# A graph-attention layer on one NeuronCore: the clearing of the accumulators, the depth of the statistics, one comparison's operand and the last batches' chunk size are changed

## The chip, the core and the metric

The kernel runs on one core of one Trainium2 chip. The metric is the device time of one execution in microseconds (us). Engines are named as in the profile: PE (TensorE, with PEld for its weight loads), DVE (VectorE), ACT (ScalarE), POOL (GpSimd) and SP (SyncE, which here only issues DMAs).

## The reference, cut to what matters

There are 12500 nodes with 128 features, and 412500 edges, sorted by target node, with 64 features each. Four heads of 32 columns attend over the edges that enter a node.

```python
h = relu(layernorm(x))                                   # per node
hw = (h @ W_node.T).reshape(n, 4, 32)
e = (edge_attr_64 @ W_edge.T).reshape(edges, 4, 32)
att = sum(concat([hw[src], hw[dst], e]) * a)             # per edge and head
att = where(att > 0, att, 0.2 * att)
m = maximum(segment_max(att, dst), 0)
ex = exp(att - m[dst])
denom = segment_sum(ex, dst) + (edges - deg) * exp(-m)
out = x + segment_sum(ex / denom[dst] * hw[src], dst)
```

## The kernel before, in words

**Node table.** The first stage normalizes the nodes and multiplies them with one prepared matrix (`wall`), and writes 98 blocks of 128 rows to `table` in HBM. A row has 144 numbers: per head 32 projected columns, two ones and the source's share of the attention, and behind them the target's shares. Blocks come in groups (3, 6, then mostly 9 blocks: one load of `xg`, one write of the table) and in units of three blocks. The order on every engine is written out by hand (`tc.manual_schedule()`): loop step `k` issues the product of unit `k` (`project`, `keep_rows`), the normalizing and the transposes of unit `k+2` (`normalize`, `turn`, `keep_turned`) and the statistics of unit `k+ahead` (`measure`). When a group's last unit is measured, the next steps take its square root on ACT (`root`, L282) and its reciprocal and shift on DVE (`deviate`, L287 and L289). Step `k == 4` issues the loads of `load_extents` (L215), and four later steps the POOL subtraction `find_rise` (L225). Ahead of the loop, the first `ahead - 2` units are measured.

**Extents.** After the table, `extent` and about 25 short DVE instructions (L230 to L444) work out where every chunk of edges begins and ends among the nodes. One result is `nid`, the node number that a partition stands for in each group of four chunks.

**Edges.** Edges come in chunks of 896 (7 tiles of 128), eight chunks to a batch, 58 batches; the last has five chunks and 31 tiles. `gather` issues one indirect DMA on POOL for each tile (L497), which fetches 128 rows of the table: 3223 in all. `hs` has two buffers. In the iteration of batch `b` the gathers of batch `b+1` are issued, then `weigh(b)` (attention, running maxima, exponentials), `scatter(b)` (rows times weights on DVE, L575; a product with the one-hot `hot` on PE, L583; `collect` copies the sums out on ACT, L606), `begin(b+1)` (edge scores of the next batch on PE), and after every second batch `merge` (into the accumulators `acc`, L653). Of the last two batches each has a merge of its own. `finish` divides, adds `x`, and writes groups of nodes that are complete.

`scatter` takes chunks in steps of `G` = 3: three chunks' rows are multiplied, then one set of matmuls has 96 columns of `hot` as weights and 420 columns to stream; in the last batch the step is 1 (32 columns as weights, 140 to stream).

`begin` starts with two DVE comparisons of 128x896 each (L510): which edges of a chunk go to which node, as ones and zeros in `mem`. The matmuls L518 then add the targets' shares. Four short instructions on DVE follow (L521 to L527), and the one-hot comparisons (L530).

One PSUM bank, named `exr`, holds small operands: the exponentials (`ex_ps`), a row of numbers (`rows_ps`) and a scratch piece for `finish` (`em_ps`).

`acc` (128x13720 numbers) is cleared by one ACT copy. It is the first statement of the edge stage (L745), but on ACT, where nothing holds it back, it stands first of all computing instructions.

Of the kernel before, what the change touches and what calls it, by code (L numbers as in the profile page):

```python
# [9 lines left out]
F32 = mybir.dt.float32  # L10
BF16 = mybir.dt.bfloat16
I32 = mybir.dt.int32
AF = mybir.ActivationFunctionType
OP = mybir.AluOpType
# [3 lines left out]
P = 128  # L18
N = 12500
D = 128  # L20
# [4 lines left out]
T = 7  # L25
CE = T * P
# [73 lines left out]
def kernel(  # L100
# [77 lines left out]
    with (  # L178
# [62 lines left out]
        def load_rows(b0, n):  # L241

            full = min(n, (N - b0 * P) // P)
            s = Rows()
            s.b0, s.n = b0, n
            s.x = p2.tile([P, XB, D], F32, name="xg", bufs=4)
            nc.sync.dma_start(s.x[:, :full, :],
                              x[b0 * P:(b0 + full) * P, :].rearrange("(b p) d -> p b d", p=P))
            if full < n:
                nc.gpsimd.memset(s.x[:, full, :], 0.0)  # L250
                rest = N - (b0 + full) * P
                nc.sync.dma_start(s.x[:rest, full, :], x[(b0 + full) * P:N, :])
            s.stats = p2.tile([P, XB, 2, 3], F32, name="stats", bufs=4)
            s.units = []
            for i0 in range(0, n, XS):
                u = Rows()
                u.s, u.i0, u.m = s, i0, min(XS, n - i0)
                s.units.append(u)
            return s


        def measure(u):
            s = u.s
            for i in range(u.i0, u.i0 + u.m):
                nc.vector.bn_stats(s.stats[:, i, :, :].rearrange("p a b -> p (a b)"), s.x[:, i, :])  # L265
            if u is not s.units[-1]:
                return

            n = s.n
            tot = p2.tile([P, XB, 2], F32, name="tot", bufs=4)  # L270
            nc.vector.tensor_tensor(tot[:, :n, :], s.stats[:, :n, 0, 1:], s.stats[:, :n, 1, 1:], op=OP.add)  # L271
            dif = p2.tile([P, XB], F32, name="dif", bufs=4)
            nc.vector.tensor_tensor(dif[:, :n], s.stats[:, :n, 0, 1], s.stats[:, :n, 1, 1], op=OP.subtract)
            nc.vector.scalar_tensor_tensor(dif[:, :n], dif[:, :n], D / 4.0, dif[:, :n], op0=OP.mult, op1=OP.mult)
            nc.vector.tensor_tensor(dif[:, :n], dif[:, :n], tot[:, :n, 1], op=OP.add)
            s.mean2, s.var = tot[:, :n, 0], dif[:, :n]
            measured.append(s)

        def root(s):
            n = s.n  # L280
            s.rstd = p2.tile([P, XB], F32, name="rstd", bufs=4)
            nc.scalar.activation(s.rstd[:, :n], s.var, AF.Sqrt, bias=eps, scale=1.0 / D)  # L282
            rooted.append(s)

        def deviate(s):
            n = s.n
            nc.vector.reciprocal(s.rstd[:, :n], s.rstd[:, :n])  # L287
            s.shift = p2.tile([P, XB], F32, name="shift", bufs=4)
            nc.vector.scalar_tensor_tensor(s.shift[:, :n], s.mean2, -0.5, s.rstd[:, :n], op0=OP.mult, op1=OP.mult)  # L289

        def normalize(u):
# [45 lines left out]
                groups.append(s)  # L337
                units.extend(s.units)

        for _ in range(4):  # L340
            load_next()
        ahead = 6
        for u in units[:ahead - 2]:
            for s in rooted:
                deviate(s)
# [18 lines left out]
        while k < len(units):  # L364
# [26 lines left out]
                find_rise(k // 4 - 4)  # L391
            k += 1
        write(full)
        pe = pps.tile([P, H], F32, name="pw", bufs=1)
        nc.tensor.matmul(pe, we.rearrange("p s k -> p (s k)"), a_diag[:, 2, :], start=True, stop=True)
        for s in range(2):
# [54 lines left out]
    ps = stack.enter_context(tc.tile_pool(name="ps", bufs=1, space=bass.MemoryType.PSUM))  # L451


    bank = ps.tile([P, T * R + W + GB * 4], F32, name="exr")
    ex_ps = bank[:, :T * R].rearrange("p (t r) -> p t r", t=T)
    rows_ps = bank[:, T * R:T * R + W]
    em_ps = bank[:, T * R + W:]
    nc.scalar.copy(rows_ps, riota)

    hot = work.tile([P, T, CB, W], F32, name="hot")  # L460

# [44 lines left out]
    def begin(s):  # L506

        for k in range(2):
            pair = 2 * s.b + k
            nc.vector.tensor_scalar(s.mem[:, k, :], s.mem[:, k, :].bitcast(I32), nid[:, pair:pair + 1], None,  # L510
                                    op0=OP.is_equal)
        s.z = ps.tile([R, CE], F32, name="z")
        for part in (slice(0, HALF), slice(HALF, CE)):
            for j in range(SB):
                nc.tensor.matmul(s.z[:, part], wa3[:, j, :], s.eft[:, j, part], start=(j == 0), stop=False)  # L515
        for part in (slice(0, HALF), slice(HALF, CE)):
            for k in range(2):
                nc.tensor.matmul(s.z[:, part], twb[:, s.b % 2, k, :], s.mem[:, k, part], start=False,  # L518
                                 stop=(k == 1))
        dk = work.tile([P, SB * CT], I32, name="dk")  # L520
        nc.vector.tensor_scalar(dk, s.dst, W - 1, None, op0=OP.bitwise_and)  # L521

        key = work.tile([P, SB * CT], F32, name="key")
        nc.vector.tensor_tensor(key.rearrange("p (c t) -> p c t", t=T), s.dst.rearrange("p (c t) -> p c t", t=T),
                                floor[:, s.b * CB:(s.b + 1) * CB, None].to_broadcast([P, CB, T]), op=OP.subtract)
        nc.vector.tensor_scalar(key, key, float(W), float(W), op0=OP.is_ge, op1=OP.mult)
        nc.vector.tensor_tensor(key, key, dk, op=OP.add)  # L527
        for q0 in range(0, s.chunks, 2):
            k = key[:, q0 * T:q0 * T + CT].rearrange("p (q t) -> p q t", t=T)
            nc.vector.tensor_tensor(hot[:, :, q0:q0 + 2, :].rearrange("p t q r -> p q t r"),  # L530
                                    rows_ps[:, None, None, :].to_broadcast([P, 2, T, W]),
                                    k[:, :, :, None].to_broadcast([P, 2, T, W]), op=OP.is_equal)
# [31 lines left out]
    def scatter(s):  # L564


        by_chunk = s.hs[:, :, :EROW].rearrange("p (q t) k -> p q t k", t=T)
        held = [n for j in range(SB) for n in tiles_of(s.b * SB + j)]
        step = G if s.b + 1 < NBT else 1
        for q0 in range(0, s.chunks, step):  # L570
            w = min(step, s.chunks - q0)
            for q in range(q0, q0 + w):
                n = held[q]
                rows = by_chunk[:, q, :n, :].rearrange("p t (h k) -> p t h k", h=H)[:, :, :, :HB]
                nc.vector.tensor_tensor(  # L575
                    rows, rows, ex_ps[:, :n, q * H:(q + 1) * H, None].to_broadcast([P, n, H, HB]), op=OP.mult)
            pa = ps.tile([P, G * H * AW], F32, name="pa", bufs=2)

            n = held[q0 + w - 1]
            order = [0, *range(n, T if w > 1 else n), *range(1, n)]  # L580
            for i in order:
                v = w if i < n else w - 1
                nc.tensor.matmul(pa[:v * W, :v * H * AW], hot[:, i, q0:q0 + v, :].rearrange("p q r -> p (q r)"), by_chunk[:, q0:q0 + v, i, :],  # L583
                                 start=(i == order[0]), stop=(i == order[-1]))
            collect(s, q0, w, pa)
# [156 lines left out]
    with tc.manual_schedule():  # L742
        for b in range(-1, NBT):
            if b == -1:
                nc.scalar.copy(acc.rearrange("p q d -> p (q d)"), carry_m.to_broadcast([P, NQ * AW]))  # L745
                for k in range(2):
                    batch(k).src, batch(k).dst = early[k]
                load_pen(batch(0))
            elif b + 2 < NBT:
                batch(b + 2).src, batch(b + 2).dst = index(b + 2)  # L750
            if b + 1 < NBT:
                load(batch(b + 1))
                gather(batch(b + 1), sums if b >= 1 else None)
            if b >= 0:
                s = batch(b)
                weigh(s)
                if b + 1 < NBT:
                    load_pen(batch(b + 1))
                for store in stores:
                    store()  # L760
                stores.clear()
                scatter(s)
            if b + 1 < NBT:
                begin(batch(b + 1))
            if b >= 0:
                first, last = merge_of(b)
                if b == last:
                    merge(first * CB, chunks_of(first, last))
                del batches[b]
            if b == 3:  # L770
                count_windows()
            for b0, n, behind in parts():
                if behind == b:
                    stores.append(finish(work, ps, "up", em_ps, b0, n))
        for store in stores:
            store()
# [251 lines left out]
```

## Time and profile before

| | |
|---|---|
| median of 3 runs | 4203.52 us (4203.04 to 4205.55) |
| profiled execution | 4203.49 us, its span 4201.7 us |
| first gather starts | 95.19 us after the span's start |
| last gather starts, ends | 4152.28, 4153.23 us |
| L497, gathers on POOL | 3223, mean 954 ns busy |
| L510, comparisons on DVE | 116, mean 672 ns |
| L745, clearing on ACT | 1, 11.62 us |
| busy shares | POOL 74%, DVE 42%, PE 37%, ACT 15% |

A row of the groups reads: line, engine, operation, output<-inputs, shapes, count, then busy time and the mean of one in ns, then the engine's idle time just before them and who ended it. A row of the timeline reads: start, duration (of all that are merged into the row), engine, line, operation, and in brackets the idle time before it and who ended that.

### The profile page before, as it was taken

The numbers are of one execution on the slowest core, as the hardware profiler recorded it, in microseconds if no ns is written. First come the engines' busy times: TensorE is split into PE (matmuls) and PEld (weight loads), VectorE is DVE, ScalarE is ACT, GpSimd is POOL, SyncE is SP. The second block draws the span as 40 slices with busy tenths as digits, with TensorE's granted clock in tenths as the row PEclk, the third lists the DMA queues.
The fourth block names the chain that finished last, engine by engine and source line by source line (L and its number), as shares of the span: only waits on it lengthen the run. The fifth ranks groups of instructions, "written<-read, shape, count | busy, mean of one in ns | idle before, by whom it ended". The sixth has DMA issues, their size and how long they took to land.

```text
span 4201.7 us, 23990 instructions
## 1 busy us (share of the span) xinstructions
PE 1537.7 (37%) x4651; PEld 630.5 (15%) x4651; DVE 1767.9 (42%) x3336; ACT 648.3 (15%) x2553; POOL 3099.8 (74%) x3337
## 2 busy tenths in 40 slices
PE   5324242424342423333333333343334242424243
PEld 4101110111111111111111111111111111111111
DVE  7334353435342534353435343534353434333445
ACT  5111111101110111111111111111111111111111
POOL 2777777777777777777777777777777777777774
PEclk9667676666666766666666667676767676767676
DMA  5333433343333333334333334333333333333331
GB/s 169 114 113 88 130 97 113 93 118 88 118 93 113 97 113 93 118 88 118 93 113 98 113 93 118 88 117 93 113 97 113 93 116 90 115 95 110 100 108 48
DMA packets 243628, 440.90 MB, mean 105 GB/s; under 512 B 93946, under 2 KB 144118, under 8 KB 243478
## 3 DMA queue, kind: packets, MB, share of 16 engines
q0 software_dynamic: 103136, 237.83, 21.6%
q1 hardware_dynamic: 127030, 194.11, 13.8%
q10 hardware_dynamic: 13312, 7.36, 0.6%
q8 instruction: 45, 0.74, 0.1%
q14 instruction: 105, 0.86, 0.1%
HBM read 423.75 MB, written 15.29 MB: 104 GB/s over the span
## 4 chain that ended last, share of the span: by engine, by line
POOL 71%; issue 24%; DVE 2%; DMA 1%; PE 1%; ACT 1%; SPq 0%; POOLq 0%; ACTq 0%; DVEq 0%
POOL hs L497 71%; DMA hs<-table,src 1%; PE pa L583 1%; DVE hT L311 0%; ACT acc L745 0%; DVE stats L265 0%; POOL gate L495 0%; DVE hn L297 0%; PE pt L306 0%; ACT hn L300 0%; PE ph L316 0%; DMA twb<-table 0%; DVE acc L653 0%; DVE tot L271 0%; ACT r L606 0%
## 5 line engine op out<-in xcount | busy, mean ns | idle before, releaser
L497 POOL DMA_INDIRECT hs<-table,src x3223 | 3073.3, 954 | 978.2 <-issue 968.1
L583 PE MATMUL pa<-hs,hot 128*96 128x420 f32 (+2 forms) x2456 | 902.1, 531 | 2465.3 <-issue 2421.5
L583 PEld LDWEIGHTS pa<-hs,hot 128*96 128x96 f32 (+2 forms) x2456 | 413.7, 173 | 2965.6 <-issue 2829.1
L538 DVE STREAM_TRANSPOSE zst<-hs 128x224 f32<-128x224 f32 x58 | 33.6, 579 | 1681.2 <-DMA hs<-table,src 1681.2
L606 ACT COPY r<-pa 32x35 f32<-32x35 f32 x1842 | 385.3, 209 | 819.0 <-PE pa L583 799.1
L575 DVE TENSOR_TENSOR hs<-hs,exr 128x924 f32<-128x924 f32 x461 | 476.8, 1102 | 0.0
L547 ACT ACTIVATE a<-z 32x224 f32<-32x224 f32 x232 | 80.5, 347 | 2087.8 <-DVE z L546 2087.8
L515 PE MATMUL z<-eft,wa 128*32 128x384 f32 (+1 forms) x928 | 361.5, 543 | 21.2 <-DMA twb<-table 21.2
L530 DVE TENSOR_TENSOR hot<-exr,key 128x448 f32<-128x448 f32 x231 | 138.7, 622 | 396.4 <-PE pa L583 394.5
L518 PE MATMUL z<-mem,twb 128*32 128x512 f32 x464 | 185.6, 543 | 5.9 <-DVE mem L510 5.9
L556 ACT ACTIVATE both<-a 32x224 f32<-32x224 f32 x232 | 89.9, 388 | 370.1 <-DVE a L553 365.8
L515 PEld LDWEIGHTS z<-eft,wa 128*32 128x32 f32 x928 | 97.6, 110 | 269.2 <-issue 269.2
L546 DVE TENSOR_TENSOR z<-z,zst 32x224 f32<-32x224 f32 x232 | 89.7, 387 | 81.6 <-ACT a L547 76.2
L653 DVE TENSOR_TENSOR acc<-acc,a 128x70 f32 x461 | 108.3, 235 | 32.9 <-DVE acc L653 18.0
L550 DVE TENSOR_TENSOR_SCAN up<-pen,z 32x896 f32<-32x896 f32 x58 | 117.0, 2016 | 2.0
L552 DVE TENSOR_TENSOR_SCAN m<-pen,up 32x896 f32<-32x896 f32 x58 | 116.4, 2007 | 2.0
L558 DVE SCALAR_TENSOR_TENSOR both<-pen,m 32x224 f32<-32x224 f32 x232 | 88.1, 380 | 2.4
L510 DVE TENSOR_SCALAR mem<-mem,nid 128x896 f32<-128x896 int32 x116 | 73.3, 672 | 21.5 <-DMA mem<-in_dstc 21.5
L718 PE MATMUL up<-a,ident 128*32 128x224 f32 (+2 forms) x480 | 44.0, 542 | 96.6 <-DVE a L711 96.6
L548 DVE TENSOR_TENSOR z<-z,a 32x896 f32<-32x896 f32 x58 | 63.0, 1087 | 24.0 <-ACT a L547 24.0
L518 PEld LDWEIGHTS z<-mem,twb 128*32 128x32 f32 x464 | 51.2, 111 | 130.9 <-issue 114.3
L553 DVE TENSOR_TENSOR a<-z,m 32x896 f32<-32x896 f32 x58 | 62.5, 1078 | 2.0
(140 smaller groups left out, 735.4 us busy)
## 6 DMA issues: line engine op xcount, KB each, us to landing
eft<-in_ef SPq DMA_DIRECT2D x58, 1792.0 KB
mem<-in_dstc SPq DMA_DIRECT2D x116, 448.0 KB
hs<-table,src POOLq DMA_INDIRECT x3223, 2.6
twb<-table SPq DMA_DIRECT2D x464, 0.5 KB
pen<-pens SPq DMA_DIRECT2D x58, 112.1 KB
xg<-in_x SPq DMA_DIRECT2D x14, 448.0 KB
table<-rows ACTq DMA_DIRECT2D x9, 648.0 KB
out<-xg SPq DMA_DIRECT2D x13, 448.0 KB
```

What stands on the lines that cost most here:

```text
L497: nc.gpsimd.indirect_dma_start(out=s.hs[:, i, :], out_offset=None, in_=table[:, :], in_offset=bass.IndirectOffsetOnAxis(ap=s.src[:, i:i + ...
L515: nc.tensor.matmul(s.z[:, part], wa3[:, j, :], s.eft[:, j, part], start=(j == 0), stop=False)
L518: nc.tensor.matmul(s.z[:, part], twb[:, s.b % 2, k, :], s.mem[:, k, part], start=False, stop=(k == 1))
L530: nc.vector.tensor_tensor(hot[:, :, q0:q0 + 2, :].rearrange("p t q r -> p q t r"), rows_ps[:, None, None, :].to_broadcast([P, 2, T, W]), k ...
L546: nc.vector.tensor_tensor(grouped(s.z, g), grouped(s.z, g), zst[g * R:(g + 1) * R, :, :], op=OP.add)
L550: nc.vector.tensor_tensor_scan(up, s.pen[:, :CE], s.z, 0.0, op0=OP.add, op1=OP.max)
L552: nc.vector.tensor_tensor_scan(m[:, ::-1], s.pen[:, CE:0:-1], up[:, ::-1], 0.0, op0=OP.add, op1=OP.max)
L556: nc.scalar.activation(both[g * R:(g + 1) * R, 0, :, :], grouped(att, g), AF.Exp)
L575: nc.vector.tensor_tensor(rows, rows, ex_ps[:, :n, q * H:(q + 1) * H, None].to_broadcast([P, n, H, HB]), op=OP.mult)
L583: nc.tensor.matmul(pa[:v * W, :v * H * AW], hot[:, i, q0:q0 + v, :].rearrange("p q r -> p (q r)"), by_chunk[:, q0:q0 + v, i, :], start=(i ...
L606: nc.scalar.copy(to, pa[q * W:(q + 1) * W, k:k + AW])
L653: nc.vector.tensor_tensor(cols, cols, put[:, i0 + i, :, :], op=OP.add)
```

## The change

Four things. The ACT copy that clears `acc` stands behind the last write of the table. The statistics run eight units ahead of the product in place of six, so six units in place of four are measured ahead of the loop; for this the five small tiles of a group have five buffers in place of four, and five groups are loaded at the start. `nid` is copied into the PSUM bank, and the two comparisons of `begin` read it there as a broadcast tensor, as a `tensor_tensor` in place of a `tensor_scalar`. And `scatter` goes by single chunks in the last two batches, not the last alone.

```diff
-            s.x = p2.tile([P, XB, D], F32, name="xg", bufs=4)
+            s.x = p2.tile([P, XB, D], F32, name="xg", bufs=5)
...
-        for _ in range(4):
+        for _ in range(5):
             load_next()
-        ahead = 6
+        ahead = 8
...
         write(full)
+        nc.scalar.copy(acc.rearrange("p q d -> p (q d)"), carry_m.to_broadcast([P, NQ * AW]))
...
-    bank = ps.tile([P, T * R + W + GB * 4], F32, name="exr")
+    bank = ps.tile([P, T * R + W + GB * 4 + NC2 // 4], F32, name="exr")
...
-    em_ps = bank[:, T * R + W:]
+    em_ps = bank[:, T * R + W:T * R + W + GB * 4]
+    nid_ps = bank[:, T * R + W + GB * 4:]
     nc.scalar.copy(rows_ps, riota)
+    nc.scalar.copy(nid_ps, nid)
...
-            nc.vector.tensor_scalar(s.mem[:, k, :], s.mem[:, k, :].bitcast(I32), nid[:, pair:pair + 1], None,
-                                    op0=OP.is_equal)
+            nc.vector.tensor_tensor(s.mem[:, k, :], s.mem[:, k, :].bitcast(I32),
+                                    nid_ps[:, pair:pair + 1].to_broadcast([P, CE]), op=OP.is_equal)
...
-        step = G if s.b + 1 < NBT else 1
+        step = G if s.b + 2 < NBT else 1
...
             if b == -1:
-                nc.scalar.copy(acc.rearrange("p q d -> p (q d)"), carry_m.to_broadcast([P, NQ * AW]))
                 for k in range(2):
                     batch(k).src, batch(k).dst = early[k]
```

`stats`, `tot`, `dif`, `rstd` and `shift` get a fifth buffer in the same way as `xg`.

More of the change, by code (lines that the diff above doesn't have):

```diff
@@ L252, in load_rows @@
                 nc.sync.dma_start(s.x[:rest, full, :], x[(b0 + full) * P:N, :])
-            s.stats = p2.tile([P, XB, 2, 3], F32, name="stats", bufs=4)
+            s.stats = p2.tile([P, XB, 2, 3], F32, name="stats", bufs=5)
             s.units = []
@@ L269, in measure @@
             n = s.n
-            tot = p2.tile([P, XB, 2], F32, name="tot", bufs=4)
+            tot = p2.tile([P, XB, 2], F32, name="tot", bufs=5)
             nc.vector.tensor_tensor(tot[:, :n, :], s.stats[:, :n, 0, 1:], s.stats[:, :n, 1, 1:], op=OP.add)
-            dif = p2.tile([P, XB], F32, name="dif", bufs=4)
+            dif = p2.tile([P, XB], F32, name="dif", bufs=5)
             nc.vector.tensor_tensor(dif[:, :n], s.stats[:, :n, 0, 1], s.stats[:, :n, 1, 1], op=OP.subtract)
@@ L280, in root @@
             n = s.n
-            s.rstd = p2.tile([P, XB], F32, name="rstd", bufs=4)
+            s.rstd = p2.tile([P, XB], F32, name="rstd", bufs=5)
             nc.scalar.activation(s.rstd[:, :n], s.var, AF.Sqrt, bias=eps, scale=1.0 / D)
@@ L287, in deviate @@
             nc.vector.reciprocal(s.rstd[:, :n], s.rstd[:, :n])
-            s.shift = p2.tile([P, XB], F32, name="shift", bufs=4)
+            s.shift = p2.tile([P, XB], F32, name="shift", bufs=5)
             nc.vector.scalar_tensor_tensor(s.shift[:, :n], s.mean2, -0.5, s.rstd[:, :n], op0=OP.mult, op1=OP.mult)
```

## The prediction

> **What bounds the kernel now.** I read the page's chain first, then the groups, then the timeline at the start, in one batch and at the end.
>
> ```profile
> POOL 71%; issue 24%; DVE 2%; DMA 1%; PE 1%; ACT 1%; SPq 0%; POOLq 0%; ACTq 0%; DVEq 0%
> L497 POOL DMA_INDIRECT hs<-table,src x3223 | 3073.3, 954 | 978.2 <-issue 968.1
> ```
>
> The chain lies on POOL and its "issue" gaps for 95%. The gathers go from 95.19 to 4153.23 us without a pause; a gather takes 0.94 us, a gap 0.30. So the time is a sum of three: 95.2 before the first gather, 3222 starts from there to 4152.28, and 48.5 us from the last start to the span's end. The median distance of two starts is 1.249 us; 3222 x 1.249 = 4024.3, but the starts span 4057.1. The missing 32.8 us are gathers that took longer. The timeline shows where:
>
> ```profile
> 2013.18 8.28 DVE L575 TENSOR_TENSOR hs<-hs,exr 128x924 f32<-128x924 f32 x8
> 2014.01 0.94 POOL L497 DMA_INDIRECT hs<-table,src  x1 [0.30 <-issue]
> ...
> 2021.39 1.25 DVE L510 TENSOR_SCALAR mem<-mem,nid 128x896 f32<-128x896 int32 x2
> 2021.50 1.36 POOL L497 DMA_INDIRECT hs<-table,src  x1 [0.30 <-issue]
> ...
> 3515.74 0.71 DVE L632 TENSOR_TENSOR r<-r,scale 128x528 f32<-128x528 f32 x1
> 3515.86 1.41 POOL L497 DMA_INDIRECT hs<-table,src  x1 [0.30 <-issue]
> ```
>
> The gather beside the comparison takes 1.36, not 0.94. I took every gather and asked which DVE instruction runs 0.13 us after its start, the point at which all the lengthened ones agree: with L510 there (60 times) it is longer by 0.37 in the mean, 22.3 us in all, and by just what is left of that one instruction (0.38 in the mean). With L632, both inputs in SBUF, 16 times 0.25: 4.1 us. With L575, one input in PSUM, 399 times: nothing; L530 and L644, of that kind too, 110 and 48 times: nothing. The rest of the 32.8 is small pieces.
>
> ```profile
> 3.95 11.62 ACT L745 COPY acc<-carry_m 128x13720 f32<-128x13720 f32 x1
> 15.59 1.28 ACT L282 ACT_TABLE_LOAD   x1
> 16.89 0.30 ACT L282 ACTIVATE rstd<-dif,eps 128x3 f32<-128x3 f32 x1
> 17.22 0.18 DVE L287 RECIPROCAL rstd<-rstd 128x3 f32<-128x3 f32 x1 [12.15 <-ACT rstd L282]
> ```
>
> At the start DVE is ready for the first root at 5.06 (L275 ends), and waits 12.15 us for ACT, which clears `acc`.
>
> **The start: clear behind the table, statistics earlier.** Without the clear, the table load of L282 begins when L275 ends, at 5.06 (the load of L556 waited for its input too), so the root ends at 5.06 + 1.28 + 0.30 = 6.65 in place of 17.19: 10.5 us. Of this the new order gives some back: two more units are measured and group 2's statistics and deviation are made ahead of the loop, and ACT takes group 2's root before the first `hn`. From the same rows: second group's statistics end at 8.95, three units (nine statistics at 0.21) and four short ones end at 12.2, `a_diag`, the two `wall` copies with PE's answer 13.5, deviation 13.9. DVE's first `hn` (21.89 before) comes at 13.9: 8.0 us gained. In the loop DVE has two units and one group's chain less, 2 x 0.67 + 1.0 = 2.3 us. It is the fullest engine there: a group takes 5.63 us (L275 at 44.34, 49.98), of which 0.47 is a wait for `pt`, because ACT's `hn` waits for a shift made in the same step (waits: ACT hn L300 <- DVE shift L289, 10.3 us in 9 times). With the shift two steps early I take that wait as gone, 9 x 0.47 = 4.2. Against it: the last eight units, not six, have no statistics, and go at PE's pace (0.7 of transposes and 0.9 of products, not DVE's 0.85): 1.5 back. And DMA: it is full (1.10, 1.02, 1.02 of 16 engines) from 34 to 49 us, when the four `dch` loads lie on the table writes; with all of it in a shorter time I give back 2. Sum 8.0 + 2.3 + 4.2 - 1.5 - 2 = 11.0 (bounds 7 and 14). The first gather waits for the last table write (issued at 90.61, 4.6 us before it), which moves with this; the DVE chain behind (L230 to L444) and the SP loads of batch 0 move as well. The fifth load costs SP one issue (0.45 to 1.2 us) in the idle start, and its 576 KB follow the other four's at the 298 GB/s that the queues move from 2.5 to 7.5 us, so they are there by 11; they are wanted at 13.9 at the earliest.
>
> The clear itself now lies on ACT behind the last write, about 79 to 91 us. Who is queued behind it: the copies into the bank, of which the later waits for `nid` anyway (115 before, about 104 now), and nothing before 150 us. It costs nothing; were that cover gone, at most 11.6. The new `nid_ps` copy is 0.2 us, ahead of a comparison that waits 17.29 us for its DMA.
>
> **The comparison.** L510 twice takes 1.25 us; as an operation with one PSUM input I cost it by L575: 8.28 / 8 = 1.035 for 924, so 1.00 for 896, 0.75 us more a batch on DVE. Behind it are queued the short key instructions and `hot` (L530), which waits for PE after that (0.97 and 4.31 us in the batch above), and L518 on PE, 16 us later. Nobody waits, and DVE idles 18 to 38 us before each L538. So DVE's loss costs nothing; if that cover were gone, 57 x 0.75 = 43 us.
>
> [...] Its row first: the lengthening is 0.40 a batch. [...] I take 22.3, less 0.4 for the last batch (below): 21.9.
>
> Some returns. Of the DVE chain in a batch nothing moves, but the gathers behind L510 come 0.42 us earlier against it. Moving every L632 by that against its gathers, and charging what is left at the 0.13 point, gives 7.4 us for 4.05: +3.3. Bounds for L632: 0, and 30 x 0.71 = 21; the shifted row is nearest. The short L521 to L527 cover the point in 58 cases at 0.00 to 0.02 us each, so nothing for them. POOL: 21.9 - 3.3 = 18.6 less (bounds 8 and 24).
>
> **Single chunks in batch 56.**
>
> ```profile
> 4131.92 14.99 PE L583 MATMUL pa<-hs,hot 128*96 128x420 f32 x42 [45.34 <-issue]
> 4146.95 1.77 ACT L606 COPY r<-pa 32x35 f32<-32x35 f32 x8 [0.78 <-PE pa L583]
> 4148.75 0.17 DVE L618 TENSOR_SCALAR mc<-r 128x8 f32<-128x8 f32 x1 [3.94 <-ACT r L606]
> 4159.72 0.57 DVE L538 STREAM_TRANSPOSE zst<-hs 128x224 f32<-128x224 f32 x1
> 4181.63 0.87 ACT L606 COPY r<-pa 32x35 f32<-32x35 f32 x4 [0.80 <-PE pa L583]
> 4183.30 1.11 ACT L606 COPY r<-pa 32x35 f32<-32x35 f32 x5 [0.80 <-PE pa L583]
> ```
>
> At the end the last gather lands near 4154.9 (2.64 after its start, as batch 27's of 1997.71 before L538 at 2000.35), but DVE takes batch 57 at 4159.72, behind merge and `finish` of batch 56. So that path sets the end, and POOL's gain in gathers of batch 57 is no gain. With single chunks PE begins after one multiplication, not three: 2.1 us earlier. A chunk costs PE 1.67 (4183.30 - 4181.63) against 4.94 / 3 = 1.65 in threes, the same. PE's slow first part was 5.5 us in batch 57 and 3.2 in batch 56; expecting between, I give back 0.6. The last copies are four in place of eight, 0.9 less. 2.1 - 0.6 + 0.9 = 2.4 us (bounds 0.5 and 3.5; the landing would be the bound only from 4.8 on).
>
> **Sum.** 11.0 + 18.6 + 2.4 = 32.0. The profiled execution's 4203.49 (1.8 outside its span) is the median to 0.03, so 4171.5 us.
>
> **The rivals.** (1) The comparison goes on holding the gather, now for longer. For it: the integer input still comes from SBUF. Against: 399 silent L575. It begins 0.24 us before the point, so 1.00 leaves 0.77 in place of 0.40: 57 x 0.37 = 21 us more; with 13.4 gained at the ends, and no shift of L632, 4211. It is slower from 0.40 + 13.4 / 57 = 0.63 us a batch; held through both comparisons, 1.77 a batch, 57 x 1.37 = 78 more, 4268. 0.06. (2) The relief is given back: the new phase puts L632 or others on the point every time (at most 21 for L632), or the start stays at DMA's pace (7): 4183 to 4195. For it: full DMA; 28 phases that I know only from the trace of before. 0.10. (3) More than I take: start 14, POOL 24, end 3.5: 4162; beyond that, under 4160. 0.04. (4) That the clear isn't moved on ACT: its place among ACT's instructions is behind the last table write, so no.
>
> **How the numbers follow.** The forecast 4171.5 with its bounds has 0.80: 7 + 8 + 0.5 = 15.5 and 14 + 24 + 3.5 = 41.5 are the corners, 4188 and 4162, and hardly all at once on the weak side; I take 4160 to 4183. The noise of three runs is under 0.2% (8.4 us): faster means below 4195.1. Rival 1 falls on both sides of 4211.9: slower 0.04, same 0.02; of rival 2, 0.02 may lie above 4195. Faster 0.80 + 0.08 + 0.04 = 0.92; same 0.04; slower 0.04.
>
> **What would show it.** First gather near 84 (95.19); L510's successor 116 times about 1.0 us and no gather beside it over 1.0; the distance of first to last start near 4038 (4057.1); L632's gathers 7 us long in all; from batch 56's L538 (4115.69) to batch 57's 41.6 us in place of 44.0, and from there to the end 42.0 as now. It is wrong if gathers beside the comparison still take 1.3 or more, or if the first gather stays later than 88.

## The result, and the profile after

The changed kernel takes 4160.3 us (median, 4160.05 to 4160.67) against 4203.5 us in the same session: ratio 0.9897, 95% interval [0.9882, 0.9911]. The profiled execution took 4160.05 us, its span 4157.8. Behind L448 every line number of the prediction is 3 higher in the changed kernel (L510 is L513, L632 is L635); the clear is L394.

The page's chain and the row of the gathers:

```profile
POOL 71%; issue 25%; DVE 2%; DMA 1%; PE 1%; ACT 0%; POOLq 0%; DVEq 0%; ACTq 0%
L500 POOL DMA_INDIRECT hs<-table,src x3223 | 3047.1, 945 | 978.2 <-issue 969.3
```

POOL is the bound as before. Its gathers have become shorter, 945 in place of 954 ns, and the issue gaps have not changed. The three pieces of the time, from the starts of the gathers in the two traces:

| | before | after | less | forecast |
|---|---|---|---|---|
| first gather starts | 95.19 | 80.25 | 14.9 | 11.0 |
| first to last start | 4057.09 | 4030.89 | 26.2 | 18.6 + 0.4 |
| last start to the span's end | 49.4 | 46.7 | 2.8 | 2.4, less 0.4 |
| sum (difference of the spans) | | | 43.9 | 32.0 |

(The prediction gives the last piece as 48.5 us; that is from the last gather's end. From its start it is 49.4, and no term depends on it. The 0.4 in the last column is what the gathers of the last batch gain: it shortens the distance of the starts, and the forecast left it out because the end waits for batch 56.)

The timeline beside the comparison, whose rows are start, duration, engine, line:

```profile
1994.73 2.07 DVE L513 TENSOR_TENSOR mem<-mem,exr 128x896 f32<-128x896 int32 x2
1994.85 0.94 POOL L500 DMA_INDIRECT hs<-table,src  x1 [0.30 <-issue]
```

The comparison is longer by 0.82 us a pair, begins at the same place, 0.12 us ahead of the gather, and the gather beside it is 0.94 long where it was 1.36. The start:

```profile
5.03 0.16 DVE L275 TENSOR_TENSOR dif<-dif,tot 128x3 f32<-128x3 f32 x1
5.28 1.28 ACT L282 ACT_TABLE_LOAD   x1 [5.28 <-DVE dif L275]
6.57 0.30 ACT L282 ACTIVATE rstd<-dif,eps 128x3 f32<-128x3 f32 x1
...
13.78 0.34 DVE L297 TENSOR_SCALAR hn<-xg,rstd,shift 128x128 f32<-128x128 f32 x1
...
36.91 0.52 ACT L323 COPY rows<-ph 128x432 f32<-128x432 f32 x1 [3.30 <-DMA table<-rows]
...
75.68 0.38 ACTq L328 DMA_DIRECT2D table<-rows  x1
76.10 11.63 ACT L394 COPY acc<-carry_m 128x13720 f32<-128x13720 f32 x1 [0.62 <-POOL rows L324]
80.25 1.12 POOL L500 DMA_INDIRECT hs<-table,src  x1 [4.59 <-DMA pens<-pen]
```

The root follows the first statistics at once, the first `hn` on DVE comes at 13.78 (21.89 before), and the clear runs on ACT after the last table write, while POOL waits for that write to land. (The gather's row names another DMA; but in before, after, e_clear and e_ahead the first gather stands 4.55 to 4.58 us behind the issue of the last table write.) At 36.91 there is a new wait: ACT can't fill a buffer of table rows, because the write out of it hasn't ended. The end of batch 56:

```profile
4074.74 0.58 DVE L541 STREAM_TRANSPOSE zst<-hs 128x224 f32<-128x224 f32 x1 [21.00 <-DMA hs<-table,src]
4088.97 15.58 PE L586 MATMUL pa<-hs,hot 128*32 128x140 f32 x112 [43.35 <-DVE hs L578]
4105.49 0.17 DVE L621 TENSOR_SCALAR mc<-r 128x8 f32<-128x8 f32 x1 [3.46 <-ACT r L609]
4111.14 0.99 POOL L500 DMA_INDIRECT hs<-table,src  x1 [0.30 <-issue]
4116.33 0.57 DVE L541 STREAM_TRANSPOSE zst<-hs 128x224 f32<-128x224 f32 x1
```

Batch 57 still begins behind `merge` and `finish` of batch 56 (no idle time ahead of its transpose), 41.59 us after batch 56 in place of 44.03.

### The profile page after: what moved, and what is told of

Read it like the earlier page. It is cut to its first block, busy times and chain, and to the rows that moved or that the text cites. A ratio compares the mean times of both kernels' runs of the same rounds, so it can differ in the third digit from the quotient of the medians.

```text
span 4157.8 us, 24120 instructions
## 1 busy us (share of the span) xinstructions
PE 1538.9 (37%) x4721; PEld 637.2 (15%) x4721; DVE 1814.1 (44%) x3336; ACT 645.9 (16%) x2553; POOL 3073.5 (74%) x3337
## 4 chain that ended last, share of the span: by engine, by line
POOL 71%; issue 25%; DVE 2%; DMA 1%; PE 1%; ACT 0%; POOLq 0%; DVEq 0%; ACTq 0%
POOL hs L500 71%; DMA hs<-table,src 1%; PE pa L586 1%; DVE stats L265 0%; POOL gate L498 0%; DVE hT L311 0%; DMA table<-rows 0%; DVE hn L297 0%; PE ph L316 0%; PE pt L306 0%; DMA pens<-pen 0%; DVE dif L274 0%; DVE acc L656 0%; DMA xg<-in_x 0%; PE up L721 0%
## 5 line engine op out<-in xcount | busy, mean ns | idle before, releaser
L500 POOL DMA_INDIRECT hs<-table,src x3223 | 3047.1, 945 | 978.2 <-issue 969.3
L513 DVE TENSOR_TENSOR mem<-mem,exr 128x896 f32<-128x896 int32 x116 | 120.3, 1074 | 18.9 <-DMA mem<-in_dstc 18.9
L561 DVE SCALAR_TENSOR_TENSOR both<-pen,m 32x224 f32<-32x224 f32 x232 | 88.0, 379 | 2.4
```

The source lines that it names most:

```text
L500: nc.gpsimd.indirect_dma_start(out=s.hs[:, i, :], out_offset=None, in_=table[:, :], in_offset=bass.IndirectOffsetOnAxis(ap=s.src[:, i:i + ...
L513: nc.vector.tensor_tensor(s.mem[:, k, :], s.mem[:, k, :].bitcast(I32), nid_ps[:, pair:pair + 1].to_broadcast([P, CE]), op=OP.is_equal)
```

## Experiments

In three sessions (e_chunk to e_best; e_delay2 to e_chunk2; e_order) all kernels, the one before too, took 5109 to 5177 us: PE stood still between its instructions there (ahead of `z` 676 us in e_chunk, 660 in e_delay), and the gathers waited for PE's sums (911 us in e_chunk, 856 in e_order). Their times are compared only with each other, and the section on what was not expected shows the rows.

**e_scalar: the old comparison alone put back.**

```diff
-            nc.vector.tensor_tensor(s.mem[:, k, :], s.mem[:, k, :].bitcast(I32),
-                                    nid_ps[:, pair:pair + 1].to_broadcast([P, CE]), op=OP.is_equal)
+            nc.vector.tensor_scalar(s.mem[:, k, :], s.mem[:, k, :].bitcast(I32), nid[:, pair:pair + 1], None,
+                                    op0=OP.is_equal)
```

> The changed kernel with the old comparison (tensor_scalar, nid in SBUF), the other three edits kept. Theory, the comparison's operand is what held the gathers: gathers beside L513 are lengthened again, about 60 times by 0.37, 22 us in all, and L635 may get back up to 3 of its 4 us, since the gathers behind move against the DVE chain; 4182 to 4186 us, first gather at 80.3 as in the changed kernel. Rival, the stretch of gathers got shorter because the whole schedule was shifted (earlier start, other phases), whatever the operand: at most 5 us lost, 4160 to 4165.

Measured: 4187.2 us, before 4203.9; this is 1.2 us above the theory's range, and far from the rival's. Its timeline, and its row of the gathers from the groups:

```profile
2007.11 1.25 DVE L513 TENSOR_SCALAR mem<-mem,nid 128x896 f32<-128x896 int32 x2
2007.24 1.35 POOL L500 DMA_INDIRECT hs<-table,src  x1 [0.30 <-issue]
```

```profile
L500 POOL DMA_INDIRECT hs<-table,src x3223 | 3073.4, 954 | 978.1 <-issue 966.8 <-DMA hs<-table,src 6.4 <-DVE ext L232 4.6
```

The gathers are 26.3 us longer in all than the changed kernel's (3073.4 - 3047.1), the distance from first to last start is 4057.09, the figure of the kernel before, and the first gather is at 80.73. The middle piece belongs to the comparison alone. With a DVE instruction assigned to each gather by the point 0.13 us behind its start, as in the prediction, L513 lengthens 58 gathers by 22.1 us, and L635, though nobody touched it, 15 gathers by 4.2 (1.06 in the changed kernel). The rival falls.

**e_sbuf: the new operation, both operands in SBUF.**

```diff
-                                    nid_ps[:, pair:pair + 1].to_broadcast([P, CE]), op=OP.is_equal)
+                                    nid[:, pair:pair + 1].to_broadcast([P, CE]), op=OP.is_equal)
```

> The changed kernel with tensor_tensor kept, but its second operand the broadcast nid in SBUF, not in PSUM: both inputs from SBUF. Theory, what counts is two reads from SBUF at the point 0.13 us into a gather: the first comparison begins 1.125 us after a gather's start, lasts 1.03, so 0.78 of it are left at the next gather's point; 57 x 0.78 = 44 us lost, 4204 us. Rival, only the operation counts (a tensor_scalar holds the gather, a tensor_tensor does not, wherever its operands are): 4160 to 4162.

Measured: 4208.3 us (the theory said 4204), ratio to before 1.0012 [1.0003, 1.0021]; first to last start 4078.9, 48 us more than in the changed kernel.

```profile
2018.28 2.07 DVE L513 TENSOR_TENSOR mem<-mem,nid 128x896 f32<-128x896 int32 x2
...
2018.43 1.74 POOL L500 DMA_INDIRECT hs<-table,src  x1 [0.30 <-issue]
```

Same operation, same 2.07 us, and the gather is 0.80 longer. 59 gathers are lengthened by 0.81 in the mean, and what was left of the one instruction at the point is 0.82. So what frees the gather here is the operand in PSUM (0.94 us beside L513 in the changed kernel, 1.74 here), not `tensor_tensor`; and although both comparisons cover 2.07 us, only the rest of the first is charged.

**e_clear and e_ahead: the two edits of the start, each alone on the kernel before.**

```diff
         write(full)
+        nc.scalar.copy(acc.rearrange("p q d -> p (q d)"), carry_m.to_broadcast([P, NQ * AW]))
...
-                nc.scalar.copy(acc.rearrange("p q d -> p (q d)"), carry_m.to_broadcast([P, NQ * AW]))
```

> The kernel before with the clear alone moved behind the last table write. Theory, the front of the start and the loop's gain are separate: DVE's first hn comes 10.5 us earlier (at 11.4), the loop keeps its 68.7 us from there to the last table write, so the first gather is at about 84.7; the stretch of gathers stays at 4057 +-2; 4193 to 4195 us. Rival, the transfers set the loop's pace once it begins earlier: first gather at 88 to 90, 4197 to 4199 us.

```diff
-            s.x = p2.tile([P, XB, D], F32, name="xg", bufs=4)
+            s.x = p2.tile([P, XB, D], F32, name="xg", bufs=5)
...
-        for _ in range(4):
+        for _ in range(5):
             load_next()
-        ahead = 6
+        ahead = 8
```

> The kernel before with the statistics alone eight units ahead (five buffers, five groups loaded); the clear stays first on ACT. Theory of the prediction (two units and a group's chain leave the loop, the wait for the shift goes): first hn at 21.9 as before, loop shorter by 6 to 7 us as in the changed kernel, first gather at 88 to 89, 4196.5 to 4198 us. Rival, the loop got shorter by the transfers' earlier begin and not by the order: first gather at 94 to 95, 4202 to 4204 us. In both the stretch of gathers stays at 4057 +-2.

| us | before | e_clear | e_ahead | after |
|---|---|---|---|---|
| median | 4203.9 | 4192.9 | 4202.3 | 4160.3 (own session) |
| first `hn` on DVE | 21.89 | 11.39 | 24.10 | 13.78 |
| from there to the last table write's issue | 68.7 | 69.5 | 62.2 | 61.9 |
| first gather | 95.19 | 85.49 | 90.82 | 80.25 |
| first to last start | 4057.1 | 4055.6 | 4058.0 | 4030.9 |

e_clear does nearly what its theory said: `hn` earlier by 10.5, the loop no shorter (0.8 longer), 0.9975 [0.9965, 0.9985] in the time. e_ahead pays 2.2 us ahead of the loop and takes 6.5 out of it; its 4.4 us at the first gather shrink to 2.7 in the span, since the other two pieces are 0.9 and 0.8 longer in that run, and to 0.9996 [0.9987, 1.0005] in the time, which is no difference that can be told. Its theory was right on the loop (6 to 7 us shorter) and wrong on the rest: it had the first `hn` where it was, the first gather at 88 to 89, and 4196.5 to 4198 us. The loop's gain comes from the order, not from an earlier begin. The two gains add up: 9.7 + 4.4 = 14.1, together 14.9.

**e_chunk and e_chunk2: single chunks in batch 56 alone.** Edit: `s.b + 1 < NBT` is `s.b + 2 < NBT` in the kernel before.

> The kernel before with single chunks in batch 56 alone. Theory: from batch 56's zst transpose to batch 57's 41.6 us in place of 44.0, from there to the end 42 us as before, the stretch of gathers 4057 +-2, first gather at 95.2; so 2.4 us less, 4201.1. Rival, the smaller products cost PE as much as the earlier begin saves, or batch 57 waits for its last gather's landing: 43 to 44 us between the two transposes, 4203 to 4204.

> The kernel before with single chunks in batch 56 alone, once more on a chip where the gathers are the bound. Theory: from batch 56's zst transpose to batch 57's 41.6 us in place of 44.0, from there to the end 42 us, the stretch of gathers 4057 +-2, so 4201 us. Rival: 43 to 44 us between the two transposes, 4203 to 4204 us.

Measured: ratios 1.0002 [0.9989, 1.0015] and 0.9992 [0.9982, 1.0002], with 54 us between the two transposes; PE's pauses hide the question in both. It is answered by the other runs, which are with and without the edit: between the transposes of batch 56 and batch 57 lie 44.0 (before), 44.4 (e_clear) and 45.3 us (e_ahead) in threes, and 41.6 (after), 42.5 (e_scalar), 41.6 (e_sbuf) and 42.7 (e_best3) with single chunks: 2.5 us in the mean. These kernels differ in other edits too, and each group spreads by 1.1 to 1.3 us; but the groups don't overlap.

**e_delay, e_delay2 and e_order: the comparison unchanged, but begun later against the gathers.** e_delay adds the memset once, e_delay2 twice.

```diff
     def begin(s):
 
+        nc.vector.memset(spare_ps, 0.0)
```

> The kernel before, tensor_scalar and SBUF operands kept, with one more DVE instruction ahead of the two comparisons: a memset of 128x228 numbers of PSUM that nobody reads (about 0.3 us), 57 times more work for DVE. Theory, only the one instruction counts that covers the point 0.13 us into a gather: the first comparison now begins just behind a gather's point and ends before the next, the second has 0.05 us left there; so 2 to 8 us of lengthening beside L510 in place of 22, and 4182 to 4190 us though DVE does more. The distance of two merges is then again about 140.0 us, not 140.8, and the scale multiplication of merge should hold the gathers by about 1 us in all, as in the changed kernel, if that distance sets it, and by about 4 if the comparison's kind does. Rival, a comparison excludes the gathers for as long as it runs, wherever it begins: 4203 to 4207 us.

> The kernel before, tensor_scalar and SBUF operands kept, with two memsets of 128x228 numbers of PSUM that nobody reads ahead of the comparisons (one shifts them by 0.16 us, as e_delay's trace shows). Theory, only the one instruction counts that covers the point 0.13 us into a gather: the first comparison now begins about 0.07 us behind a gather's point and ends before the next, of the second 0.02 to 0.1 us are left there; 1 to 6 us of lengthening beside L510 in place of 22, and 4182 to 4190 us though DVE does more. The distance of two merges is then again about 140.0 us, not 140.8, and the scale multiplication of merge should hold the gathers by about 1 us in all, as in the changed kernel, if that distance sets it, and by about 4 if the comparison's kind does. Rival, a comparison excludes the gathers for as long as it runs, wherever it begins: 4203 to 4207 us.

```diff
     def begin(s):
 
+        dk = work.tile([P, SB * CT], I32, name="dk")
+        nc.vector.tensor_scalar(dk, s.dst, W - 1, None, op0=OP.bitwise_and)
+
+        key = work.tile([P, SB * CT], F32, name="key")
+        nc.vector.tensor_tensor(key.rearrange("p (c t) -> p c t", t=T), s.dst.rearrange("p (c t) -> p c t", t=T),
+                                floor[:, s.b * CB:(s.b + 1) * CB, None].to_broadcast([P, CB, T]), op=OP.subtract)
```

> The kernel before, tensor_scalar and SBUF operands kept and no work added: the two key instructions L521 and L524 stand ahead of the two comparisons and not behind them, so the comparisons begin 0.37 us later against the gathers. Theory, only the one instruction counts that covers the point 0.13 us into a gather: the first comparison begins about 0.25 into a gather and ends before the next one's point, of the second 0.06 to 0.15 us are left there; 4 to 9 us of lengthening beside L510 in place of 22, 4185 to 4191 us. Rival, a comparison in this form costs the gathers a fixed time wherever it begins: 20 us or more beside L510, 4202 to 4206 us.

Measured: 1.0001 [0.9990, 1.0011], 0.9994 [0.9979, 1.0009] and 0.9992 [0.9982, 1.0002]. POOL waits 0.9 ms for PE in such a session (856 us at `gate` in e_order), so a freed gather is not seen in the time, and in e_delay one memset moved the comparison by 0.16 us, less than the 0.25 it needs. The expectations are neither met nor refuted. Beside the comparison the gathers are 7.5 us longer in e_order and 2.2 in e_delay2, which is what the theory gave, but in e_chunk and e_chunk2, where the comparison was left as it was, they are only 9.9 and 6.8 us longer, so these sums decide nothing. What can be read is single places, as this of e_delay2:

```profile
2882.93 0.62 DVE L510 MEMSET exr<- 128x228 f32 x2
2883.08 1.11 POOL L498 DMA_INDIRECT hs<-table,src  x1 [0.31 <-issue]
2883.45 1.20 DVE L513 TENSOR_SCALAR mem<-mem,nid 128x896 f32<-128x896 int32 x2
2884.49 0.99 POOL L498 DMA_INDIRECT hs<-table,src  x1 [0.30 <-issue]
```

The comparisons begin 0.37 into a gather; the next gather's point, 2884.62, finds 0.03 of the second left (it ends at 2884.65), and that gather is 0.04 longer, not 0.42. But the gather beside the memsets is 0.17 longer, which the theory did not have.

**e_best, e_best2 and e_best3: the changed kernel with three buffers for table rows, and `scale` of `merge` in PSUM.**

```diff
-                s.rows = p2.tile([P, XB, ROW], F32, name="rows")
+                s.rows = p2.tile([P, XB, ROW], F32, name="rows", bufs=3)
...
-        scale = work.tile([P, MC], F32, name="scale")
+        scale = scale_ps
```

> The changed kernel with two more edits: three buffers for the table rows in place of two, and merge's scale in PSUM. Theory: ACT's waits for the table writes (4.0 us in 2) go, the first gather comes 1 to 2.4 us earlier; no gather beside L635 is lengthened, 1.06 us; 4156.8 to 4158.2 us. Rival for the start, the transfers are what sets the pace from 20 to 40 us, so the wait moves to the loads: first gather at 80.0 to 80.5, 4159 to 4160 us.

> The changed kernel with three buffers for the table rows and merge's scale in PSUM, once more on a chip where the gathers are the bound. Theory: first gather about 1.9 us earlier than the changed kernel's 80.25, as the run of e_best showed, and 1.06 us less lengthening beside L635: 4156.8 to 4158 us. Rival: the lengthening comes back beside other instructions and the start is the same: 4160 us.

> The changed kernel with three buffers for the table rows and merge's scale in PSUM, a third time. Where the gathers are the bound (the kernel before at 4203 us): first gather 1.0 to 2.2 us earlier than the changed kernel's, as on the other chips, no lengthening beside L635 (1.06 us), 4156.8 to 4158.2 us. Where PE's instructions come late (the kernel before above 5100 us): the start's and the operands' gain is not seen in the time, ratio 0.998 to 1.000 to the kernel before.

Measured: 0.9987 [0.9976, 0.9997] and 0.9991 [0.9978, 1.0005] in the sessions with PE's pauses, although all of the change is in it; then 4160.8 us, 0.9889 [0.9873, 0.9906], in a session in which the kernel before took 4207.4. Against the changed kernel (0.9897) no difference can be told, where 2 to 4 us less were expected. In e_best3 the start is 1.8 better (first gather at 78.49), and groups of the loop go by without a wait for the table write:

```profile
35.17 0.17 DVE L275 TENSOR_TENSOR dif<-dif,tot 128x9 f32<-128x9 f32 x1
...
40.12 0.17 DVE L275 TENSOR_TENSOR dif<-dif,tot 128x9 f32<-128x9 f32 x1
...
45.06 0.17 DVE L275 TENSOR_TENSOR dif<-dif,tot 128x9 f32<-128x9 f32 x1
```

No gather beside the scale multiplication is longer (1.06 us in the changed kernel). But 55 gathers beside L562 (`both`, both inputs in SBUF; L561 in the changed kernel) are now lengthened by 3.3 us in all, where it was 0.6. In the changed kernel it runs at the point of a gather hardly less often, but there it begins ahead of that gather's start in 15 of 46 cases, in e_best3 in 48 of 55. What that means is shown in the next section, at L632. The stretch is 1.9 us longer, the end 1.3, and the gain is given back.

## Why the prediction was right, and where its terms were off

**The comparison (21.9 forecast).** Right: 22.3 us beside L510 became 0. e_scalar brings them back (22.1), and e_sbuf shows that the operand's place decides: 0.81 us a gather with the same operation. The prediction took the size from the rows of the trace before, and they held: a `tensor_tensor` with two SBUF inputs does hold the gather (59 times in e_sbuf), and what is charged is the rest of one instruction (0.82 us), not the whole of both (2.07). But its rule did not ask whether the instruction begins ahead of the gather or behind its start (see L632 below). Which part of the gather's work is held, no run here shows. Rival 1 (held on, 0.77 a batch in place of the 0.40 that L510 cost in the trace before) is what e_sbuf does: it forecast 4211, and e_sbuf, which has the edits of both ends, took 4208.

**What DVE pays (nothing).** Right. L513 takes 1074 ns where 1000 were costed (672 before), 46 us more on DVE, and the stretch does not show it.

**L632 (+3.3 forecast, -3.0 measured).** The step that failed: "charging what is left at the 0.13 point". To run at that point is not enough to hold a gather. Already the trace of before has an instruction with both inputs in SBUF that does so at no cost, L558 of `weigh`; in e_best3 the same instruction, L562, holds its gather:

```profile
180.01 0.94 POOL L497 DMA_INDIRECT hs<-table,src  x1 [0.30 <-issue]
180.09 0.38 DVE L558 SCALAR_TENSOR_TENSOR both<-pen,m 32x224 f32<-32x224 f32 x1
```

```profile
653.04 0.38 DVE L562 SCALAR_TENSOR_TENSOR both<-pen,m 32x224 f32<-32x224 f32 x1
653.20 1.04 POOL L501 DMA_INDIRECT hs<-table,src  x1 [0.30 <-issue]
```

The first begins 0.08 us behind the gather's start and runs 0.33 past the point, and the gather takes its usual 0.94. The second begins 0.16 ahead, has 0.09 left at the point, and the gather is 0.10 longer. This holds throughout the seven traces of kernels that took 4160 to 4208 us (before, after, e_scalar, e_sbuf, e_clear, e_ahead, e_best3). From 130 us on, one of three instructions (the comparison with both operands in SBUF, the scale multiplication, `both`) runs alone at the point of 638 gathers and beyond it. In 453 of these it had begun 0.07 us or more ahead of the gather: the gather is longer by 0.35 us in the mean, and each by what was left, to 0.02. In 185 it began between 0.03 ahead and 0.13 behind: 0.36 us were left in the mean, and no gather is longer by more than 0.01. e_order has it for the comparison too: six that begin 0.002 to 0.016 us ahead of a gather, with 0.53 left at the point, cost nothing. So in these traces a gather waited for an instruction that had been running for 0.07 us or more when it started, and not for one that began 0.03 ahead of it or later (behind a memset it was otherwise, see the last section). The author's estimate of the border is 0.05, between the two. Charged at the point alone, every L632 moved by 0.42 gives the prediction's 7.4; charged only where it began more than 0.05 ahead, the same move gives 1.7. That is 2.4 us less than the 4.1 of before, where 3.0 less came.

The other 0.6 lies in "Of the DVE chain in a batch nothing moves". The chain moves against the gathers from batch to batch. From the batch's transpose (L538) to L632 it is 35.0 to 36.4 us before, down by 0.1 to 0.6 with each merge and up again by 1.1 after three or four. In the changed kernel it is 35.05 to 35.14 in the first eight merges, jumps once, and creeps from 36.57 to 36.30 in the next 17. Three of these in its timeline:

```profile
2080.10 0.71 DVE L635 TENSOR_TENSOR r<-r,scale 128x528 f32<-128x528 f32 x1
...
2360.04 0.71 DVE L635 TENSOR_TENSOR r<-r,scale 128x528 f32<-128x528 f32 x1
2361.13 0.94 POOL L500 DMA_INDIRECT hs<-table,src  x1 [0.30 <-issue]
...
2500.01 0.71 DVE L635 TENSOR_TENSOR r<-r,scale 128x528 f32<-128x528 f32 x1
2501.12 0.94 POOL L500 DMA_INDIRECT hs<-table,src  x1 [0.30 <-issue]
```

From the second to the third it is 139.97 us. Both stand just behind the point of their gather, and are over before the next one's, which is not touched (0.94). The chain moves with PE. In every batch its first products go at half pace, spaced by 0.70 us (in threes), then by 0.35. In the kernel before this slow part lasts 2.9 to 5.7 us, and over successive pairs of batches it goes 4.3, 3.6, 2.9, 5.0, 4.3, 3.6, 2.9, 5.0. The shorter this part, the earlier L632: 2.9 goes with 35.0 us behind the transpose, 5.0 with 36.1. The slow part is that of the granted clock. In six traces (before, after, e_scalar, e_sbuf, e_clear, e_ahead) the record of the clock is made of stretches at 0.5 and at 1.0, whose lengths are whole multiples of 3.4133 us (150 stretches before, 140 after), and in each of 56 batches the slow part ends within 0.4 us of a rise to 1.0. Two batches are 140.9 us before, 41 x 3.4133 us and 0.98 us, so the slow part changes with each pair; they are 139.99 after, 41 x 3.4133 us and 0.04 us, so it stays. In e_sbuf, with 141.7 (41.5 x 3.4133 us), L635 stands at two places in turn. At about 140.9 us (before, e_scalar, e_clear, e_ahead) the scale multiplication costs 4.1, 4.2, 2.5 and 4.0 us, at 139.99 it costs 1.1 and in e_sbuf 1.0. The way the phases move goes with the distance of two batches in all six. That the cost does too is not shown: the four have the `tensor_scalar` and the two have the `tensor_tensor`, and a kernel in which the distance alone is changed was not run.

**The start (11.0 forecast, 14.9 measured).** The front's 8.0 was right: the first `hn` comes 8.1 earlier, 10.5 by the clear (e_clear) less 2.2 by the order (e_ahead). What was mis-sized is the loop, 2.3 + 4.2 - 1.5 - 2 = 3.0 forecast and 6.8 measured (68.7 to 61.9). Where the 3.8 lie can only be estimated. "9 x 0.47 = 4.2": a group without the wait for `pt` is shorter by 0.70, not 0.47 (5.64 us before, 49.98 to 55.62; 4.94 in e_best3, 40.12 to 45.06 above), since DVE's busy time falls as well, from 5.00 to 4.80. For nine groups that would be 6.3; but e_best3 has only three as short. "1.5" for two more units without statistics: from the last statistics to the last table write it is 9.9 us for six such units before and 12.5 for eight after, so two cost 2.6, and 2.6 - 2 x 0.85 = 0.9; e_scalar, with the same start, has 13.9 for eight, which makes it 2.3, so this term is not settled. The give-back to the transfers stands: ACT's wait for the table write came (3.30 at 36.91), and e_best3, without it, is 1.8 better, where 2 were given back. 2.3 + 6.3 - 0.9 - 1.8 = 5.9 of the 6.8; the rest stays open.

**The end (2.4 forecast).** 2.44 between the transposes, 2.5 in the mean of seven runs. No cost of the clear behind the table is seen: in e_clear the stretch of gathers and the end are 1.5 and 1.1 us shorter than before.

**The sum.** 11.0, 18.6 and 2.4 were 32.0; 14.9, 26.2 and 2.8 came. The time lies inside the range by 0.3 us, at its low end, where rival 3 stands ("start 14, POOL 24, end 3.5"). That it lies inside at all is luck: start and POOL both went beyond the bounds that the prediction gave them (7 to 14, 8 to 24). They were taken for the less likely side because of two sizes: 3.3 for L632, which had the wrong sign, and 3.0 for the loop.

## What to carry to other kernels

A DVE instruction of no weight on DVE can cost the engine that is the bound (here 78 us of DVE's time cost POOL 22.3): look for the same instruction beside the lengthened row each time, and try one of its two inputs in PSUM even if it then takes longer (here 1074 ns in place of 672, and the 22.3 us went). In the seven traces counted here, such an instruction cost something only where it was already running when the other engine's instruction started (453 gathers of 638): count it so, and test such a rule on all rows of the old trace that should obey it, the silent ones too. Phases between engines are not a constant of the program: here the record of PE's clock changes at whole multiples of 3.4133 us, and with two batches 0.9 us shorter the collisions fell elsewhere (L632's 4.1 us became 1.1), so give such terms both signs and a wide bound, not the phases of the old trace shifted. And before a gain of a stall is counted, see that the stalled engine is the bound in the session that is timed.

## What was not expected

**PE's pauses.** In three sessions the kernel before took 5124 to 5164 us in the median. Two answers of the waits follow, each row with the total, the times and the longest: first the kernel before at 4203 us, then e_chunk (the same program up to batch 56) in such a session, PE's and POOL's.

```profile
PE z L515 <- DMA twb<-table: 21.2, 1, 21.2
```

```profile
PE z L515 <- issue: 676.4, 377, 21.4
PE z L518 <- issue: 199.8, 139, 4.6
```

```profile
POOL gate L495 <- ACT sums L593: 910.9, 56, 39.7
```

At 4203 us L515 waits once. In e_chunk PE stands 377 times ahead of it for nothing that the profile shows, and POOL's gathers wait for PE's sums through `gate`, 16 us a batch. (The page of e_chunk puts 41% of its chain down to a releaser that the profile can't name, so PE's part in the chain is not shown in full.) There a change to POOL's path is worth next to nothing: e_best, with all of the change in it, gained 5 us there and 47 in another session on the same chip. What stops PE there was not found.

**A memset of PSUM ahead of a comparison.** It has no input in SBUF, and yet it changes what the gathers pay. Of ten gathers of e_delay2 that have a memset at the point, six are not longer; four are by 0.61 to 0.62 us, which is what is left of the comparison that begins behind the memset, 0.13 to 0.14 us after the gather's start. In e_delay 17 comparisons that begin 0.02 to 0.10 us after a gather's start, right behind a memset, hold it by 0.50 to 0.58 us, where such late ones cost nothing without a memset. And 22 gathers of e_delay2 are longer by 0.08 to 0.28 us in the way of the one shown above, between memset and comparison. Why is open.
